# Stage work paced by TensorE time beside a selective scan: equal shares, three slots, two of them ahead of the spread

## The chip, the cores and the metric

The kernel runs on one core of one Trainium2 chip. The metric is the time of one execution in device microseconds; lower is better. The time shown for the kernel before is the median of three executions.

## The reference

The input is `x` of shape (4, 96, 64, 64) in float32: four images of 96 channels. Four layers follow each other, and each computes `x = x + f(group_norm(x))`.

- Layer 0 is an attention of three heads over half-sized samples, with a 3 x 3 neighbourhood part and a 5 x 5 depthwise convolution.
- Layers 1 and 3 hold a two-dimensional selective scan in four directions (rows and columns, forwards and backwards). For 192 channels `d`, 16 states `n` and 4096 positions `t` it computes

```
h[d,n,t] = exp(delta[d,t] * A[d,n]) * h[d,n,t-1] + (delta[d,t] * u[d,t]) * B[n,t]
y[d,t]   = sum over n of h[d,n,t] * C[n,t]
```

  Around the scans stand projections, depthwise convolutions, layer norms and gates.
- Layer 2 is a 3 x 3 sharpening convolution.

## The kernel before, in words

All of it is one program of the function `streams`. Eight scans follow each other, in the order of `SCANS`: layer 1 and layer 3 for each of the four images. Beside each scan, the program computes a *stage* of an image (`BESIDE`): `first` (layer 0 and the front of layer 1), `second` (the rest of layer 1, layer 2 and the front of layer 3), `third` and `last` (the rest of layer 3). The first stage of image 0 runs before all scans. Scans 0, 3 and 4 have a `first` beside them; scans 1, 2, 5 and 6 a `second`; scan 7 has three `third` and the `last`.

**Units.** A scan is cut into groups (a direction, a stretch of 1024 positions, one half of the channels), and a group into 12 units of 8 channels x 16 states = 128 partitions and 1024 positions. There are 8 x 32 x 12 = 3072 units, 384 in each scan. What a unit `i` needs is done by small functions:

- `fetch(i)` (SyncE, SP): a DMA that spreads 8 rows of `dd` (delta) over 128 partitions, into `rep`.
- `decays(i)` (ScalarE): `rep = exp(rep * A)`, line 1952.
- `drive(i)` (TensorE): the *spread*, two bf16 matmuls of 512 columns with a 0/1 matrix `spread`, which put delta * u, held as three bf16 `parts`, on 128 partitions in the PSUM tile `bx`. There are two `bx` tiles, so `drive(i + 2)` can begin when `scan(i)` is done with its own.
- `times_b(i)` (VectorE, line 1965): `bx = bx * B`, in place.
- `scan(i)` (VectorE, line 1972): the recurrence along 1024 positions, into `hs`; `carry_on(i)` (ScalarE, line 1980) keeps its last column.
- `times_c(i)` (GpSimd, line 1984): `rep = hs * C`.
- `collect(j)` (TensorE): for three units at once, the sum over states into the PSUM tile `acc`: 6 float32 matmuls of 32 rows. A unit in which it is issued is called *due*.
- `output(j)` (VectorE or ScalarE, lines 2011 to 2017): takes `acc` to `yo` at a group's end.

`prepare(g)` computes what group `g` needs (`dd`, the products with B and C, and `parts`) while the group ahead of it runs. It is a generator: it issues a piece, then gives control back. The stages are generators too. Their pieces come in pairs: a piece of TensorE work (`yield`), then its *evacuation* from PSUM by ScalarE, VectorE or both (`yield` with a cost). A convolution gives control back between its matmuls, too (`yield (1,)`). All PSUM tiles of stages come from `bank()`: two buffers (`one`), of which `held()` keeps one for as long as a sum needs it.

**The order.** The program's order is written out by hand (`manual_schedule`): each engine executes its instructions in the order in which `unit(i, prep, work, budget)` issues them. `Slots.begin` issues the next piece of a generator, as far as a budget allows; `Slots.end` issues its evacuation. Before the change, the main loop gives each unit a budget in abstract pieces:

```
PACE = {"first": 3.5, "second": 3.7, "third": 3.2}
owed = min(owed, 0.5) + PACE[BESIDE[s][0][0]] - (2.1 if i % 3 == 1 else 0.0)
```

and `unit` issues, in this order: the fetch for unit i + 4; a first slot (preparation, in its first three slots, or else stage work); `decays(i + 2)`; `scan(i)`; `carry_on(i - 1)`; `times_c(i)`; `collect` in a due unit; `drive(i + 2)`; then, if budget is left, the first slot's evacuation and a second slot; `times_b(i + 1)`; `output`; and the remaining evacuations. So the second slot's matmuls stand behind the spread, and where there is a second slot of stage work, the first one's evacuation stands between `scan(i)` and `times_b(i + 1)`.

Near a scan's end, `work.run()` issues what is left of the stage at once.

Of the kernel before, what the change touches and what calls it, by code (L numbers as in the profile page):

```python
# [10 lines left out]
BF16 = mybir.dt.bfloat16  # L11
# [9 lines left out]
R, N = 6, 16  # L21
# [6 lines left out]
CH = 1024  # L28
NCH = L // CH
PCH = 512  # L30
# [8 lines left out]
          (("first", 3),), (("second", 2),), (("second", 3),), (("third", 0), ("third", 1), ("third", 2), ("last", 3)))  # L39
GN_EPS = 1e-5  # L40
PHI_EPS = 1e-12


PHI_SAFE = 10.0
# [850 lines left out]
def streams(ctx: ExitStack, tc: tile.TileContext, x, wts, cst, out, wat, cat, flag):  # L895
# [4 lines left out]
    keep = ctx.enter_context(tc.tile_pool(name="keep", bufs=1))  # L900
# [39 lines left out]
    spread = keep.tile([128, 4, 128], BF16, name="spread")  # L940
# [4 lines left out]
    def img(t):  # L945
        return t.rearrange("p (a b) -> p a b", b=W)

    def mm(o, lhsT, rhs, first=True, last=True):
        nc.tensor.matmul(o, lhsT=lhsT, rhs=rhs, start=first, stop=last)  # L949

    solo = [True]
# [859 lines left out]
              for k, axis, back in KINDS[tag] for c in range(NCH) for h in range(2)]  # L1811
    carry = keep.tile([128, 2, NG], F32, name="carry")
    sums = keep.tile([96, len(SCANS), 4, 2, 2 * NCH], F32, name="sums")
    cuts = [keep.tile([128, 6, PCH], BF16, name=f"parts{n}") for n in range(2)]
    for t in cuts:
        nc.gpsimd.memset(t, 0.0)
    low, ready, live = {}, {}, {}
# [21 lines left out]
    def prepare(g):  # L1839
# [83 lines left out]
        def to_parts():  # L1923
            for q in range(4):
                nc.sync.dma_start(
                    out=parts[32 * q : 32 * q + 24],
                    in_=du[:, :, bass.ts(q % 2, PCH)].rearrange("(s m d) r x -> m (d r) s x", m=2, d=8)[q // 2])

        later(1, to_du)
        later(3, to_parts)  # L1930
# [23 lines left out]
    def drive(i):  # L1954

        g, m = place(i)
        parts = ready[g][0]
        bx = ps.tile([128, CH], F32, tag="bx", name="bx")
        for e in range(2):
            mm(bx[:, bass.ts(e, PCH)], spread[:, 2 * (m % 2) + e, :], parts[:, m // 2, :])  # L1960
        live[i].append(bx)

    def times_b(i):
        bx = live[i][1]
        nc.vector.tensor_mul(bx, bx, ready[i // NG][2][:, 0, :])  # L1965
# [16 lines left out]
    def times_c(i):  # L1982
        a, hs = live[i]
        nc.gpsimd.tensor_tensor(a, hs, ready[i // NG][2][:, 1, :], ALU.mult)  # L1984
# [35 lines left out]
        return lambda: nc.sync.dma_start(out=dst, in_=yo)  # L2020

    AHEAD, BEHIND, LEAD = 4, 2, 6
    PACE = {"first": 3.5, "second": 3.7, "third": 3.2}
    total = len(groups) * NG
    per = total // len(SCANS)
    store, waiting, stored, owed = [], [], [0], 0.0
# [12 lines left out]
    def unit(i, prep, work, budget):  # L2039


        if i + AHEAD < total:
            fetch(i + AHEAD)
        while store:
            store.pop()()
            stored[0] += 1
        catch_up(1)
        j = i - BEHIND - 2
        due = j >= 0 and j % 3 == 0
        first_, rest = (prep, work) if 1 <= prep.slots <= 3 else (work, idle)  # L2050
        budget -= first_.begin(budget)
        if i + 2 < total:
            decays(i + 2)
        scan(i)
        if i:
            carry_on(i - 1)
        times_c(i)
        if due:
            collect(j)
        if i + 2 < total:  # L2060
            drive(i + 2)
        if first_ is work and budget > 0.9:
            rest = work
        if rest is not idle:
            first_.end()
            budget -= rest.begin(budget)
        if i + 1 < total:
            times_b(i + 1)
        if due and j % NG == NG - 3:
            store.append(output(j))  # L2070
        first_.end()
        rest.end()
        if first_ is not prep:
            prep.begin(0)
            prep.end()
        return budget

    class Slots:

# [1 line left out]
        def __init__(self, stage):  # L2081
            self.stage, self.open, self.slots = stage, False, 0

        def begin(self, budget):

            if budget < 0:
                return 0
            self.slots += 1
            used = 0
            v = next(self.stage, 0)  # L2090
            if v == WAIT:
                return budget
            while isinstance(v, tuple):
                used += v[0]
                if used >= budget:
                    return used
                v = next(self.stage, 0)
            self.open = v is None
            return used + (1 if self.open else v)

        def end(self):
            if self.open:
# [16 lines left out]
    with tc.manual_schedule():  # L2119
        for _ in prepare(0):  # L2120
            catch_up(9)
        catch_up(9)
        prep = Slots(prepare(1))
        for _ in range(LEAD):
            prep.begin(0)
            prep.end()
            catch_up(1)
        for i in range(AHEAD):
            fetch(i)
        decays(0)  # L2130
        decays(1)
        drive(0)
        drive(1)
        times_b(0)
        for i in range(total):
            s, at = divmod(i, per)
            g, m = divmod(i, NG)
            if at == 0:
                work, owed = Slots(beside(s)), 0.0
            if m == NG - LEAD and g + 2 < len(groups):  # L2140
                prep.run()
                prep = Slots(prepare(g + 2))

            if at == per - NG - LEAD - 1 and s < len(SCANS) - 1:
                work.run()

            owed = min(owed, 0.5) + PACE[BESIDE[s][0][0]] - (2.1 if i % 3 == 1 else 0.0)
            owed = unit(i, prep, work, owed)
        for j in range(total - 3, total, 3):
            collect(j)  # L2150
            output(j)()
            stored[0] += 1
# [51 lines left out]
```

## Time and profile before

| | |
|---|---|
| time, median of 3 runs | 14,391.75 us (14,391.1 to 14,398.4) |
| profiled execution | 14,400.5 us, span 14,398.6 us |
| granted TensorE clock, mean | 0.866 |
| before the first scan instruction / after the last | 690.6 us / 126.7 us |
| busy: TensorE, VectorE, GpSimd, ScalarE | 84%, 81%, 71%, 61% |
| DMA queue of SP, share of the 16 engines | 73.2% |
| scans 0 to 7, us each | 1632, 1656, 1666, 1634, 1629, 1659, 1669, 2037 |

The page is one execution taken by the profiler. A group's line gives the source line, engine, operation, tiles (written <- read), shapes and count, then busy time in us and the mean duration of one in ns, then idle time of the engine just ahead of these instructions and what ended it. Line 949 is the helper `mm`: all matmuls carry it, and are told apart by their tiles. A line of waits reads: who waited, for whom, us in total, times, longest us. A busy TensorE is not TensorE at its peak, since matmuls are pipelined and the ends of their spans are modelled.

### The profile page before, as it was taken

To read this page: it belongs to the slowest core of one execution; us is meant where nothing else is said; L and a number is where in the kernel's file an instruction comes from. 1 tells how busy PE (TensorE), PEld (TensorE's weight loads), DVE (VectorE), ACT (ScalarE), POOL (GpSimd) and SP (SyncE) were. 2 spreads that over 40 slices of the span, in tenths; PEclk is the share of its full clock that TensorE was granted. 3 is DMA by queue.
4 is the path that set the end of the run, shared out by engine and by line. 5 is a ranking of instruction groups with operands and counts; after the bars stand their busy time and mean duration, and the time that the engine had idled before them with its cause. 6 is when DMAs were issued, how large, how long until landed. Compare 5 with 4: busy or idle time off the path is not lost. (4 is left out here: it accounts for less than half of the span.)

```text
span 14398.6 us, 127507 instructions
## 1 busy us (share of the span) xinstructions
PE 12060.6 (84%) x40149; PEld 3562.9 (25%) x40802; DVE 11655.5 (81%) x7509; ACT 8713.8 (61%) x12340; POOL 10204.6 (71%) x4636
## 2 busy tenths in 40 slices
PE   8888887988889797889878887988979887777776
PEld 2322321322223222222222222222313222111111
DVE  1488898888878888889888898888888888778776
ACT  3266575557756676665766566566756667665554
POOL 0177886877868777778877787777868778666564
PEclk9889997998889897989879898898979888777777
DMA  0277787787877878778877788787877878677674
GB/s 9 64 174 179 193 216 198 187 207 187 223 178 199 205 200 209 180 174 206 223 185 178 186 209 219 176 207 186 212 186 197 209 190 220 168 179 173 161 184 111
DMA packets 902736, 2644.48 MB, mean 184 GB/s; under 512 B 107104, under 2 KB 257088, under 8 KB 902048
## 3 DMA queue, kind: packets, MB, share of 16 engines
q1 hardware_dynamic: 901392, 2634.72, 73.2%
q8 instruction: 324, 5.31, 0.2%
q14 instruction: 364, 2.98, 0.1%
q10 hardware_dynamic: 656, 1.46, 0.0%
HBM read 2169.16 MB, written 466.62 MB: 183 GB/s over the span
## 5 line engine op out<-in xcount | busy, mean ns | idle before, releaser
L1984 POOL TENSOR_TENSOR rep<-hs,bc 128x1024 f32<-128x1024 f32 x3072 | 7221.1, 2356 | 3057.2 <-DVE hs L1972 2499.8
L1972 DVE TENSOR_TENSOR_SCAN hs<-rep,carry,bx 128x1024 f32<-128x1024 f32 x2304 | 5401.7, 2344 | 266.0 <-ACT carry L1980 12.2
L1965 DVE TENSOR_TENSOR bx<-bx,bc 128x1024 f32<-128x1024 f32 x3072 | 3723.7, 1212 | 852.5 <-PE bx L949 432.9
L1952 ACT ACTIVATE rep<-rep,l_decay 128x1024 f32<-128x1024 f32 x3072 | 3495.7, 1143 | 519.9 <-DMA rep<-dd 502.7
L949 PE MATMUL bx<-parts,spread 128*128 128x512 bf16 x5491 | 1938.0, 429 | 1589.5 <-DVE hs L1972 1522.7
L949 PE MATMUL acc<-rep,ct 128*32 128x512 f32 x12288 | 2439.7, 703 | 16.0 <-POOL rep L1984 11.2
L1972 DVE TENSOR_TENSOR_SCAN hs<-rep,bx 128x1024 f32<-128x1024 f32 x768 | 1754.6, 2285 | 139.0 <-ACT carry L1980 47.8
L949 PEld LDWEIGHTS <-spread 128*128 128x128 bf16 x6144 | 426.0, 100 | 4080.5 <-DVE hs L1972 2610.9
L949 PE MATMUL one<-band,dg 96*96 96x512 f32 x2304 | 1048.0, 592 | 4.0
L949 PE MATMUL one<-upad,diag 96*96 96x512 f32 x2016 | 949.2, 607 | 3.8
L949 PEld LDWEIGHTS acc<-rep,ct 128*32 128x32 f32 x12288 | 492.2, 123 | 1676.0 <-issue 1401.2
L949 PE MATMUL one<-qq,kk 96*128 96x512 f32 x1152 | 684.4, 678 | 114.4 <-ACT ex L1288 75.2
L1288 ACT ACTIVATE ex<-one 128x512 f32<-128x512 f32 x576 | 342.4, 594 | 580.4 <-PE one L949 573.9
L949 PE MATMUL one<-pr,ct 6*96 6x512 f32 x1024 | 621.3, 690 | 78.6 <-DVE V L1193 10.4
L1952 ACT ACT_TABLE_LOAD x495 | 635.1, 1283 | 80.5 <-DMA rep<-dd 72.3
L949 PE MATMUL one<-hp,diag 96*96 96x512 f32 x1152 | 578.2, 642 | 31.3 <-POOL diag L1113 28.6
L1980 ACT COPY carry<-hs 128x1 f32<-128x1 f32 x2304 | 408.7, 177 | 287.0 <-DVE hs L1972 285.4
L949 PE MATMUL one<-vpad,diag 96*96 96x512 f32 x1200 | 559.2, 601 | 1.9
L949 PE MATMUL held<-ex,cols 128*32 128x256 f32 x3072 | 518.8, 415 | 8.0 <-ACT ex L1288 1.2
L949 PE MATMUL held<-ex,vT 128*32 128x256 f32 x3072 | 519.1, 415 | 0.0
L949 PEld LDWEIGHTS one<-band,dg 96*96 96x96 f32 x2304 | 374.6, 163 | 489.8 <-issue 423.7
L949 PEld LDWEIGHTS one<-upad,diag 96*96 96x96 f32 x2016 | 336.7, 167 | 438.9 <-issue 378.2
(3421 smaller groups left out, 14154.2 us busy)
## 6 DMA issues: line engine op xcount, KB each, us to landing
rep<-dd SPq DMA_DIRECT2D x3072, 512.0 KB
parts<-du SPq DMA_DIRECT2D x1024, 144.0 KB
bc<-rows SPq DMA_DIRECT2D x256, 512.0 KB
dd<-delta SPq DMA_DIRECT2D x256, 384.0 KB
du<-cut SPq DMA_DIRECT2D x256, 384.0 KB
us<-urow SPq DMA_DIRECT2D x128, 384.0 KB
du<-cut SPq DMA_DIRECT2D x256, 192.0 KB
yrow<-yo SPq DMA_DIRECT2D x128, 384.0 KB
```

The lines of the kernel that those rows point to most:

```text
L949: nc.tensor.matmul(o, lhsT=lhsT, rhs=rhs, start=first, stop=last)
L1288: nc.scalar.activation(last.rearrange("p a b -> p (a b)"), p, AF.Exp, scale=HD**-0.5)
L1952: nc.scalar.activation(a, a, AF.Exp, scale=decay[tag][:, k, NG * h + m : NG * h + m + 1])
L1965: nc.vector.tensor_mul(bx, bx, ready[i // NG][2][:, 0, :])
L1972: nc.vector.tensor_tensor_scan(out=hs, data0=a, data1=bx, initial=carry[:, h, m : m + 1] if c else 0.0, op0=ALU.mult, op1=ALU.add)
L1980: nc.scalar.copy(carry[:, h, m : m + 1], live[i][1][:, CH - 1 : CH])
L1984: nc.gpsimd.tensor_tensor(a, hs, ready[i // NG][2][:, 1, :], ALU.mult)
```

## The change

It has three parts.

- **Budget.** `mm` counts the TensorE time of each matmul at full clock (`spent`). A unit's budget is now a number of microseconds per scan (`PACE`), of which the spread (`DRIVE`) and, in a due unit, the sum (`SUM`) are taken off first. `Slots.begin` takes what its piece really issued, at least 0.5 us for each unit of cost; it issues nothing below 0.3 us of budget, and cuts a convolution where the next matmul would go over it.
- **Order.** A unit has up to three stage slots (preparation takes the place of the first in its first three slots). The first stands where it stood. `times_b(i + 1)` comes right after `times_c(i)`, and only then the first evacuation and the second slot; then `collect` and `drive(i + 2)`; then the second evacuation, the third slot, `output`, and the last evacuation. Where preparation isn't first, it has its slot at the end whatever the budget.
- **Rows.** `parts` changes from [128, 6, 512] to [128, 3, 1024]: four channel groups of 8 on four partition quarters, rather than two groups times two halves of the columns. Its loads have 72 rows of 2048 bytes each where they had 144 of 1024.

```diff
+PACE = (3.08, 3.54, 3.54, 3.08, 3.08, 3.54, 3.54, 3.4)
...
+    spent = [0.0]
+
     def mm(o, lhsT, rhs, first=True, last=True):
+
+        n = 1
+        for d in rhs.shape[1:]:
+            n *= d
+        m = o.shape[0]
+        passes = 1 if rhs.dtype == BF16 else 1.33 if m == 32 else 2 if m == R + 2 * N else 4
+        spent[0] += n * passes / 2400
         nc.tensor.matmul(o, lhsT=lhsT, rhs=rhs, start=first, stop=last)
...
-    cuts = [keep.tile([128, 6, PCH], BF16, name=f"parts{n}") for n in range(2)]
+    cuts = [keep.tile([128, 3, CH], BF16, name=f"parts{n}") for n in range(2)]
...
-                    in_=du[:, :, bass.ts(q % 2, PCH)].rearrange("(s m d) r x -> m (d r) s x", m=2, d=8)[q // 2])
+                    in_=du.rearrange("(s m d) r x -> m (d r) s x", m=4, d=8)[q])
...
-            mm(bx[:, bass.ts(e, PCH)], spread[:, 2 * (m % 2) + e, :], parts[:, m // 2, :])
+            mm(bx[:, bass.ts(e, PCH)], spread[:, m % 4, :], parts[:, m // 4, bass.ts(e, PCH)])
...
-    PACE = {"first": 3.5, "second": 3.7, "third": 3.2}
+    DRIVE, SUM, SLOT = 0.43, 1.71, 0.5
...
         due = j >= 0 and j % 3 == 0
-        first_, rest = (prep, work) if 1 <= prep.slots <= 3 else (work, idle)
-        budget -= first_.begin(budget)
+        left = budget - DRIVE - (SUM if due else 0.0)
+        mine = 1 <= prep.slots <= 3
+        left -= prep.begin(1.0) if mine else work.begin(left)
         if i + 2 < total:
             decays(i + 2)
         scan(i)
         if i:
             carry_on(i - 1)
         times_c(i)
+        if i + 1 < total:
+            times_b(i + 1)
+        if mine:
+            prep.end()
+        work.end()
+        left -= work.begin(left)
         if due:
             collect(j)
         if i + 2 < total:
             drive(i + 2)
-        if first_ is work and budget > 0.9:
-            rest = work
-        if rest is not idle:
-            first_.end()
-            budget -= rest.begin(budget)
-        if i + 1 < total:
-            times_b(i + 1)
+        work.end()
+        left -= work.begin(left)
         if due and j % NG == NG - 3:
             store.append(output(j))
-        first_.end()
-        rest.end()
-        if first_ is not prep:
-            prep.begin(0)
+        work.end()
+        if not mine:
+            prep.begin(1.0)
             prep.end()
-        return budget
+        return left
...
-        def begin(self, budget):
-
-            if budget < 0:
-                return 0
+        def begin(self, left):
+
+            if left < 0.3:
+                return 0.0
             self.slots += 1
-            used = 0
+            t = spent[0]
             v = next(self.stage, 0)
             if v == WAIT:
-                return budget
+                return left
             while isinstance(v, tuple):
-                used += v[0]
-                if used >= budget:
-                    return used
+                if spent[0] - t + 0.4 > left:
+                    return spent[0] - t
                 v = next(self.stage, 0)
             self.open = v is None
-            return used + (1 if self.open else v)
+            return max(spent[0] - t, SLOT * (1 if self.open else v))
...
-            owed = min(owed, 0.5) + PACE[BESIDE[s][0][0]] - (2.1 if i % 3 == 1 else 0.0)
+            owed = min(owed, 0.6) + PACE[s]
             owed = unit(i, prep, work, owed)
```

## The prediction

> **What bounds the kernel now.** I read the busy shares first, then the costliest groups, the stretches, and last VectorE's list of waits.
>
> ```profile
> PE 12060.6 (84%) x40149; PEld 3562.9 (25%) x40802; DVE 11655.5 (81%) x7509; ACT 8713.8 (61%) x12340; POOL 10204.6 (71%) x4636
> ...
> L1972 DVE TENSOR_TENSOR_SCAN hs<-rep,carry,bx 128x1024 f32<-128x1024 f32 x2304 | 5401.7, 2344 | 266.0 <-ACT carry L1980 12.2
> L1965 DVE TENSOR_TENSOR bx<-bx,bc 128x1024 f32<-128x1024 f32 x3072 | 3723.7, 1212 | 852.5 <-PE bx L949 432.9
> ```
>
> There are 3072 units, and each puts one scan (2344 ns) and one product (1212 ns) on VectorE: 3.56 us. From scan start to scan start the median is 3.60 us, the mean 4.42 us (13,581 us from the first scan at 690.6 to the last one's end at 14,271.9). TensorE's 84% is busy time at a clock of 0.87; its work is less than that. So a unit is a VectorE rhythm of 3.60 us with holes in it.
>
> The stretches of three of the eight scans (the first, second and last 384 units):
>
> ```profile
> 690.60:2322.20 1631.60, 1371.11 (x5463) 412.79 (x5556) 1401.11 (x852) 1026.73 (x1490) 1272.62 (x572) 0.87 0.78 195
> 2322.20:3977.90 1655.70, 1423.67 (x4256) 427.90 (x4332) 1403.80 (x868) 1056.92 (x1454) 1268.29 (x571) 0.89 0.79 198
> 12234.50:14271.90 2037.40, 1520.53 (x3861) 365.14 (x3928) 1598.03 (x1132) 1205.34 (x1701) 1267.88 (x593) 0.76 0.69 171
> ```
>
> Columns: stretch, length, busy PE, PEld, DVE, ACT, POOL, granted clock, DMA share. VectorE idles about 230, 252 and 439 us in them. Over all eight, its busy time is 11,446 us, so the holes are 2135 us. What ended them:
>
> ```profile
> DVE bx L1965 <- PE bx L949: 432.9, 281, 11.8
> DVE bx L1965 <- PE acc L949: 350.4, 175, 8.0
> DVE yo L2011 <- PE acc L949: 159.9, 77, 6.6
> DVE V L1193 <- PE one L949: 118.0, 48, 9.9
> DVE x L1600 <- ACT one L1599: 100.3, 32, 6.9
> ```
>
> Summed from the whole list: (A) `times_b` waiting for a late spread, 790 us; (B) `output` waiting for the sum, 215; (C) stage evacuations on VectorE waiting for TensorE, 385; (D) the same waiting for ScalarE, 255; (E) the rest 123. What remains, 367 us, is 0.12 us in each unit ahead of the scan, and stays.
>
> How a spread gets late shows in the timeline of the first scan:
>
> ```profile
> 1005.13 1.09 PE L949 MATMUL one<-pr,ct 6*96 6x512 f32 x2
> 1009.07 2.02 PE L949 MATMUL one<-pr,ct 6*96 6x512 f32 x2
> 1011.02 1.03 PE L949 MATMUL bx<-parts,spread 128*128 128x512 bf16 x2
> 1020.71 1.23 DVE L1965 TENSOR_TENSOR bx<-bx,bc 128x1024 f32<-128x1024 f32 x1 [4.91 <-PE acc L949]
> ```
>
> The same pair takes 1.09 us and then 2.02: the clock has halved. TensorE falls behind and VectorE loses 4.91 us.
>
> **What the Trainium skill says.** "TensorE: Matmul & The Clock Gate", part 3 (packing small matmuls), says matmuls start and end in strict program order: a spread waits for whatever stage matmul stands ahead of it. The trace agrees (the spreads run in issue order). Its part 1 (the HAM clock gate) says too little activity halves the clock. The trace shows the doubling above, and stretches of 24 units with a clock of 1.00 where TensorE has 3.7 to 3.9 us of counted work per unit, but 0.66 where it has 1.2. "DMA: Bandwidth & Descriptors", Specifications, gives 512 B as enough for line rate; here the trace differs: packets of 1024 B take 94 ns, of 2048 B 106 ns, so halving the packet count saves nearly half the time. The measurement decides.
>
> **The change part by part.** I counted each unit's matmuls from the instruction order of both programs, at the change's own rate (512 bf16 columns 0.21 us, a 512-column f32 matmul 0.85 us, a sum 1.71 us). Totals are the same: 1111 us in the first scan, 1215 in the second, 1039 in the last. Matmul, weight-load, VectorE and GpSimd counts are equal; the ScalarE table loads in the program fall by 36 of 4105, at 1.28 us each 46 us of an engine that is 61% busy, so nothing.
>
> 1. *Equal shares.* A unit with a sum has on average 3.73 us of counted work in the second scan and one without 2.88 now; then 3.36 and 3.07. Blocks of 24 units reach 3.9 now, 3.66 then. Units over 4.2 us fall from 14% to 3%. That sits at the 3.60 us rhythm where it used to stand above. In the first scan, whose attention part has the half-clock example, a block's peak drops only from 3.45 to 3.10.
> 2. *Two slots ahead of the spread.* Stage matmuls behind the spread of their unit fall from 239 to 35 us in the first scan, 232 to 41 in the second, 283 to 84 in the last; slots opened there from 153 to 33, 99 to 25, 224 to 83. Now the evacuation of such a slot stands on VectorE right after `times_b`, 1.2 us after the scan's end, while its matmul can only begin after the spread (0.4 to 0.6 us) and takes 0.85 or more: it nearly always waits. In the new order, TensorE does this work while the scan runs.
> 3. *`times_b` ahead of the evacuations.* Today 346 VectorE stage operations, in 252 units, stand between scan and `times_b`; then 4. Each gives its matmul (or TensorE and then ScalarE) 1.2 us more.
> 4. *Rows of 2048 B.* 1024 loads of `parts` at 144 packets become 72. 147,456 x 94 ns / 16 = 870 us of the queue engines becomes 73,728 x 106 / 16 = 490. The page's DMA share is 73%; TensorE waited for `parts` only 40 us in all. Bounds 0 to 40; I take 10.
> 5. *Preparation always takes its slot*, whatever the budget, and its ScalarE part now follows `times_b`; GpSimd gets its part of it no later than before. Cover: `prepare` runs over a group ahead (12 units, some 45 us). Nothing.
> 6. *What the moves put behind a wait.* `collect` and the spread now stand behind slot 2. Where slot 2 needs what slot 1's evacuation frees, the spread waits too. It has a cover of about 3.1 us: it can start when scan i ends, and is needed when scan i+1 ends (3.6 us, less its 0.5). The stores of `yo` and SP's fetches move with their units and wait for no more.
>
> **The sum.** No row shows the new order, so I choose shares between none and all of each group. (A) -40%, as equal shares remove the peaks of the second kind of scan, but not the half clock of attention: -316 (bounds +300, if slot 2 holds up spreads, to -650). (B) -30%: `output` now follows three slots, but its sum stands behind slot 2: -65 (+60 to -170). (C) and (D) -55%: slots behind the spread fall to about a third, and what is left are chains such as the layer norm's root: -352 (-100 to -520). (E) with the rows -20. Together -753. The profiled execution took 14,400.5 us (span 14,398.6); 8.8 above the median of the runs, 14,391.75. So 13,640.
>
> As a check by stages: a second-kind scan would lose 100 of 1656 (its first 48 units from 5.6 to about 4.8 us, the two blocks near 4.7 to about 4.1), a first-kind one 70 of 1632, the last one 150 of 2037: 4 x 100 + 3 x 70 + 150 = 760.
>
> **Rivals.**
> *Only the order helps.* The clock dips of attention decide (A); a slower, even pace leaves TensorE idle more often, so dips don't get rarer. (A) and (B) stay, (C) and (D) give 350: about 14,040. For it: the stall of 4.91 us above came at a block average under 3.3.
> *Nearly all holes close.* A pace below the rhythm with 3.1 us of cover leaves hardly a late spread: (A) -80%, (B) -50%, (C) and (D) -75%: -632, -107, -480, less 30: 13,140. For it: the 24 units from 3884 us on, with little stage work, run at 3.60 us in all but a few. Against it: GpSimd is busy 3.31 us and DMA 3.4 (then about 3.3) per unit, so little is left between four engines.
> *Slower: slot 2 holds the spread.* TensorE stops at slot 2's matmul until slot 1's evacuation frees its bank or writes its operand, and that evacuation now follows `times_b`. 709 units open two or more stage slots. If the wait takes 1.2 us (`times_b`) and one evacuation of 0.7 beyond the cover, 709 x 1.9 = 1350 against -753: 14,990. It decides from 1.06 us a unit on. Against it: most pairs are evacuated by ScalarE, before the scan ends, and depend on an earlier unit.
> *The shares change little.* Stage work is the same, TensorE late as before, and evacuations wait behind `times_b` for as long: 14,390.
>
> **How the numbers follow.** The sum as worked out 0.42 (13,640); only the order 0.24; nearly all holes 0.18; no difference 0.03; slower 0.13. Within 0.2% is what a measurement of this kernel can't tell from no change. Faster 0.84, same 0.03, slower 0.13. The range reaches from the case of most holes closed to the small gain with half of it lost, 13,150 to 14,280; slower than that is left out, as is the better half of the best case.
>
> **What would show it.** In the changed kernel's profile: the median from scan to scan still 3.60 us, the mean about 4.18; VectorE busy unchanged near 11,650 and its share about 86%; its waits for `bx` and `acc` together about 480 instead of 790, those of `V`, `x` and the other stage tiles together under 300 instead of 640; TensorE's idle time before `bx` for `hs` (1522.7) clearly down; the last scan under 1900 us; the clock of the second-kind scans above 0.89; DMA time of 1024 B packets gone. It is wrong if `times_b` waits as long or longer while stage waits fall (dips or slot 2), or if TensorE's waits for stage evacuations ahead of spreads grow by more than 700 us.

## The result and the profile after

The changed kernel takes 14,302.5 us (median of 4 runs, 14,296.3 to 14,315.9), the kernel before 14,392.2 beside it. The ratio is 0.9938, interval 0.9921 to 0.9955: 90 us faster, where 752 had been forecast (13,640, with a range from 13,150 to 14,280). The profiled execution took 14,307.7 us, its span is 14,305.9.

Lines in the changed kernel stand 10 higher in number (the product is L1975, the scan L1982). Busy times, and the two groups that make the rhythm:

```profile
PE 11985.5 (84%) x40137; PEld 3529.3 (25%) x40802; DVE 11649.8 (81%) x7509; ACT 8688.1 (61%) x12304; POOL 10200.4 (71%) x4636
...
L1982 DVE TENSOR_TENSOR_SCAN hs<-rep,carry,bx 128x1024 f32<-128x1024 f32 x2304 | 5401.1, 2344 | 285.5 <-ACT carry L1990 26.2
L1975 DVE TENSOR_TENSOR bx<-bx,bc 128x1024 f32<-128x1024 f32 x3072 | 3721.1, 1211 | 863.1 <-PE bx L959 501.9
```

VectorE's work is the same to a few us, and the median from scan to scan is still 3.60 us. The same three stretches (first, second and last 384 units; columns as before):

```profile
689.20:2337.90 1648.70, 1382.26 (x5467) 409.65 (x5560) 1398.56 (x851) 1026.84 (x1492) 1271.71 (x572) 0.87 0.77 193
2337.90:3975.90 1638.00, 1414.93 (x4254) 425.72 (x4332) 1401.95 (x868) 1053.41 (x1449) 1268.41 (x571) 0.89 0.79 200
12167.00:14178.60 2011.60, 1514.42 (x3860) 355.60 (x3930) 1597.25 (x1132) 1188.93 (x1685) 1266.83 (x593) 0.76 0.69 173
```

The first scan grew by 17 us, the second shrank by 18, the last by 26; the clock reads the same in each of the three. VectorE's waits:

```profile
DVE bx L1975 <- PE bx L959: 501.9, 325, 15.0
...
DVE bx L1975 <- PE acc L959: 220.4, 82, 11.9
DVE x L1610 <- ACT one L1609: 131.9, 31, 6.4
DVE yo L2021 <- PE acc L959: 99.0, 75, 6.8
DVE V L1203 <- PE one L959: 78.5, 35, 7.0
```

The product waits as long as before: its two lines come to 722 us (783 before), but with what the profile puts down to other releasers all its idle time is 833 us (822 before). `yo` and `V` wait less, but `x`, the gate that ends a chain of stage work, waits more. The changed kernel took back in one place what it gained in another, and two stretches of the second scan show it. They are its units 48 to 168 (convolutions over `band`) and 216 to 288 (mostly gates: convolution over `hp`, two projections, multiplication), in the kernel before,

```profile
2590.24:3079.80 489.56, 470.85 (x1478) 155.98 (x1501) 430.27 (x256) 297.89 (x437) 391.51 (x171) 0.98 0.81 200
3279.38:3594.19 314.81, 279.18 (x815) 84.06 (x831) 256.41 (x152) 216.99 (x277) 239.64 (x109) 0.90 0.72 183
```

and in the changed one:

```profile
2596.26:3050.15 453.89, 446.79 (x1433) 148.08 (x1458) 422.38 (x245) 288.58 (x422) 391.96 (x172) 1.00 0.85 210
3255.60:3597.04 341.44, 286.30 (x815) 83.83 (x831) 259.07 (x157) 228.90 (x304) 238.22 (x105) 0.86 0.67 173
```

The convolutions went from 4.08 to 3.78 us a unit and to a clock of 1.00: equal shares do what they should, though a part may come from 3% fewer matmuls in these units (1433 for 1478). The gates, with the same number of matmuls (815), went from 4.37 to 4.74.

One of those gate units, in the timeline of the changed kernel (VectorE's, ScalarE's and the deciding TensorE lines, 3346 to 3356 us):

```profile
3346.88 2.35 DVE L1982 TENSOR_TENSOR_SCAN hs<-rep,carry,bx 128x1024 f32<-128x1024 f32 x1
...
3347.71 0.68 ACT L1597 ACTIVATE x<-one,wt 96x512 f32<-96x512 f32 x1
...
3348.65 1.06 PE L959 MATMUL one<-x,wt 96*48 96x512 f32 x2
3349.14 1.21 DVE L1975 TENSOR_TENSOR bx<-bx,bc 128x1024 f32<-128x1024 f32 x1
3349.35 1.28 ACT L1962 ACT_TABLE_LOAD   x1
...
3350.64 1.15 ACT L1962 ACTIVATE rep<-rep,l_decay 128x1024 f32<-128x1024 f32 x1
...
3351.78 0.68 ACT L1603 ACTIVATE g<-one,wt 48x512 f32<-48x512 f32 x1
...
3352.51 2.02 PE L959 MATMUL one<-g,l_ag 48*96 48x512 f32 x2 [2.80 <-ACT g L1603]
...
3354.46 1.03 PE L959 MATMUL bx<-parts,spread 128*128 128x512 bf16 x2
3354.56 0.65 ACT L1609 ACTIVATE one<-one,der 96x512 f32<-96x512 f32 x1 [2.11 <-PE one L959]
...
3355.25 0.69 DVE L1610 SCALAR_TENSOR_TENSOR x<-one,x 96x512 f32<-96x512 f32 x1 [4.90 <-ACT one L1609]
3355.86 2.33 DVE L1982 TENSOR_TENSOR_SCAN hs<-rep,carry,bx 128x1024 f32<-128x1024 f32 x1
```

Read it backwards from the second scan. It comes 8.98 us after the first, because the multiplication of `x` stands ahead of it on VectorE. That multiplication waited 4.90 us for the `tanh` on ScalarE; this one for the second projection on TensorE; that for `g`; and `g` stood on ScalarE behind a table load (1.28 us) and the decays (1.15). Two projections of one chain were issued in one unit, so VectorE paid for the whole round through TensorE and ScalarE. TensorE stood too (2.80 us), and the spread behind the projection came late. By the time at which they ran, 22 of the 32 second projections stood in one unit with the first in the kernel before, at a mean of 7.66 us a unit, and 31 of 32 in the changed one, at 9.08. A long unit catches more of its neighbours' work, so this is a symptom; how many were issued together is counted further down.

### The profile page after: what moved, and what is told of

Same layout as the page of the kernel before. It is cut to its first block, busy times and chain, and to the rows that moved or that the text cites. A ratio compares the mean times of both kernels' runs of the same rounds, so it can differ in the third digit from the quotient of the medians.

```text
span 14305.9 us, 127489 instructions
## 1 busy us (share of the span) xinstructions
PE 11985.5 (84%) x40137; PEld 3529.3 (25%) x40802; DVE 11649.8 (81%) x7509; ACT 8688.1 (61%) x12304; POOL 10200.4 (71%) x4636
## 4 chain that ended last, share of the span: by engine, by line
PE 45%; DVE 17%; ACT 13%; DMA 8%; POOL 7%; issue 7%; SPq 1%; DVEq 0%; POOLq 0%; ACTq 0%; another core or an unknown queue 0%
PE one L959 28%; DVE hs L1982 10%; PE acc L959 8%; PE bx L959 7%; DVE bx L1975 5%; DMA rep<-dd 4%; POOL rep L1994 4%; ACT rep L1962 3%; PE held L959 2%; ACT L1962 1%; ACT L1904 1%; ACT ex L1298 1%; ACT delta L1902 1%; DMA yc<-ycol 1%; ACT cut L1924 1%
## 5 line engine op out<-in xcount | busy, mean ns | idle before, releaser
L1982 DVE TENSOR_TENSOR_SCAN hs<-rep,carry,bx 128x1024 f32<-128x1024 f32 x2304 | 5401.1, 2344 | 285.5 <-ACT carry L1990 26.2
L1975 DVE TENSOR_TENSOR bx<-bx,bc 128x1024 f32<-128x1024 f32 x3072 | 3721.1, 1211 | 863.1 <-PE bx L959 501.9
L959 PE MATMUL acc<-rep,ct 128*32 128x512 f32 x12288 | 2359.0, 688 | 18.1 <-POOL rep L1994 15.1
L1982 DVE TENSOR_TENSOR_SCAN hs<-rep,bx 128x1024 f32<-128x1024 f32 x768 | 1754.0, 2284 | 102.1 <-ACT carry L1990 22.7
L959 PEld LDWEIGHTS <-spread 128*128 128x128 bf16 x6144 | 456.2, 101 | 3350.5 <-DVE hs L1982 1832.1
```

What stands on the lines that cost most here:

```text
L1982: nc.vector.tensor_tensor_scan(out=hs, data0=a, data1=bx, initial=carry[:, h, m : m + 1] if c else 0.0, op0=ALU.mult, op1=ALU.add)
```

## The experiments

Eighteen kernels follow. The times are medians of 4 to 20 runs, and each ratio is to the kernel before as it ran beside that kernel (14,375 to 14,392 us). The columns after the ratio sum VectorE's idle time from the first scan to the end of the last, every operation of the trace counted (the prediction's groups A to D are sums of list rows, so A is 822 here and not 790): (A) ahead of the product, nearly all of it late spreads, (B) `output`, (C) stage work waiting for TensorE, (D) for ScalarE. Then comes the length of the last scan. The last column counts, in the order of instructions, pairs of stage pieces of which the second needs the result of the first and both are issued in one unit: of 190 pairs, at the eight places that `e13_two_chain` marks, those with both evacuations between the same two `decays` on ScalarE, or the same two scans on VectorE.

| kernel | us | ratio to before | A | B | C | D | last | pairs |
|---|---|---|---|---|---|---|---|---|
| before | 14,392 | | 822 | 220 | 394 | 265 | 2037 | 46 |
| changed | 14,303 | 0.9938 [0.9921, 0.9955] | 833 | 150 | 295 | 310 | 2012 | 122 |
| e1_rows | 14,380 | 0.9992 [0.9984, 0.9999] | 823 | 228 | 391 | 267 | 2036 | 46 |
| e2_order | 14,016 | 0.9742 [0.9725, 0.9760] | 847 | 161 | 169 | 167 | 1867 | 46 |
| e3_budget | 14,445 | 1.0039 [1.0027, 1.0052] | 669 | 230 | 516 | 328 | 2049 | 93 |
| e4_spread_first | 14,560 | 1.0118 [1.0099, 1.0138] | 774 | 196 | 498 | 367 | 2120 | 122 |
| e5_price | 14,280 | 0.9922 [0.9905, 0.9938] | 857 | 181 | 296 | 278 | 1975 | 132 |
| e6_two | 13,998 | 0.9734 [0.9718, 0.9750] | 768 | 186 | 175 | 211 | 1856 | 68 |
| e7_price_two | 14,171 | 0.9852 [0.9835, 0.9868] | 759 | 235 | 202 | 264 | 1852 | 94 |
| e8_free_only | 14,174 | 0.9849 [0.9832, 0.9865] | 877 | 114 | 264 | 235 | 1969 | 111 |
| e9_three_ahead | 14,308 | 0.9942 [0.9926, 0.9959] | 858 | 139 | 284 | 302 | 2001 | 122 |
| e10_two_behind | 14,388 | 0.9995 [0.9988, 1.0002] | 725 | 241 | 474 | 292 | 2043 | 68 |
| e11_two_shares | 14,196 | 0.9866 [0.9849, 0.9882] | 745 | 241 | 199 | 266 | 1862 | 94 |
| e12_two_free | 14,107 | 0.9808 [0.9790, 0.9826] | 840 | 188 | 176 | 199 | 1884 | 89 |
| e13_two_chain | 13,916 | 0.9678 [0.9662, 0.9694] | 765 | 181 | 166 | 166 | 1863 | 0 |
| e14_three_chain | 14,126 | 0.9832 [0.9815, 0.9848] | 713 | 183 | 260 | 262 | 2007 | 4 |
| e15_two_chain_more | 13,930 | 0.9688 [0.9671, 0.9704] | 744 | 223 | 149 | 120 | 1849 | 0 |
| e16_two_high | 14,079 | 0.9796 [0.9780, 0.9812] | 732 | 265 | 164 | 238 | 1850 | 60 |
| e17_three_chain_more | 14,061 | 0.9787 [0.9760, 0.9814] | 717 | 190 | 270 | 179 | 1973 | 0 |
| e18_two_chain_low | 13,876 | 0.9658 [0.9631, 0.9685] | 736 | 161 | 150 | 158 | 1849 | 0 |

In the expectations the letters are theories, which each text explains; the groups of the table are always in brackets here.

### The three parts of the change, one at a time

`e1_rows` is the kernel before with the rows alone:

```
-    cuts = [keep.tile([128, 6, PCH], BF16, ...
+    cuts = [keep.tile([128, 3, CH], BF16, ...
```

> The kernel before with the rows of parts at 2048 bytes and nothing else. All theories: 5 to 15 us less than before (TensorE waited 40 us for parts in all), so 14,380. If the transfers were worth more than their waits, over 40 us.

Measured: 12 us (1 to 23). The rows are worth about what the forecast gave them (10).

`e2_order` is the kernel before with the new order of a unit; it keeps two slots, the old budgets and the old rows:

```
         times_c(i)
+        if i + 1 < total:
+            times_b(i + 1)
...
         work.end()
+        if mine or budget > 0.9:
+            budget -= work.begin(budget)
         if due:
             collect(j)
         if i + 2 < total:
             drive(i + 2)
```

> The kernel before with the new order alone: times_b right behind times_c, and the second slot ahead of the sum and the spread, under the old budgets of at most two slots. Theory 1 (chains: a second piece that reads what the first piece's evacuation writes holds the spread back, TensorE idles and its clock halves): VectorE's waits for stage pieces fall by 100 us or more, its waits for spreads rise by as much or more in chains; 14,350 to 14,550. Theory 2 (clock: dips come from the pace, whatever the order): waits for spreads as before, stage waits down, 14,250 to 14,300. Theory 3 (clumps of pieces without matmuls, let in by their price of 0.5 us): none here, 14,250.

Measured: 376 us faster, more than any of the three theories had. (C) and (D) fall from 659 to 336, (B) by 59. (A) rises by 25.

`e3_budget` keeps the old order and takes only the new prices and equal shares (raised to 3.25, 3.62 and 3.5, so that no work is left over at the end of a scan):

> The new budgets alone, in the old order with two slots (the shares raised to 3.25, 3.62 and 3.5 us so that two slots still empty the stages). Theory 1: the convolutions gain as in the changed kernel (some 200 us of holes), no chain is made worse: 14,150 to 14,230. Theory 2: the even pace brings as many dips as it takes peaks away: 14,350 to 14,450. Theory 3: the clumps are here too, with two slots rather than three: 14,250 to 14,350, with the group norms' units slower than before.

Measured: 53 us slower, which is in the range of theory 2, but not by its mechanism, since the spreads come less late: (A) falls by 153 while (C) and (D) grow by 185; in this order the evacuations stand ahead of the product, and a longer wait there can cover part of a late spread, so the two may not be separate gains and losses. In sum the order gives 376, and with it in place the rest of the change (budgets, third slot and rows) takes 287 back. By the profiles, half of these 287 lie in the first seven scans (143), half in the last (145).

`e4_spread_first` is the changed kernel with the spread ahead of slot 2:

```
         work.end()
-        left -= work.begin(left)
         if due:
             collect(j)
         if i + 2 < total:
             drive(i + 2)
-        work.end()
+        left -= work.begin(left)
+        work.end()
         left -= work.begin(left)
```

> The changed kernel with the sum and the spread moved ahead of the second slot; all else as changed. Theory 1: the spread no longer stands behind a piece that waits, chains fall back to the holes of before, the convolutions keep theirs: 14,050 to 14,200, waits for spreads under 600 us. Theory 2: same as the changed kernel or slower, since late evacuations come back: 14,300 to 14,400. Theory 3: 14,300, the group norm's clumps as in the changed kernel.

Measured: 258 us slower than the changed kernel. Slot 2 does hold some spreads up ((A) falls by 59), but behind the spread its evacuation makes VectorE wait for TensorE ((C) and (D) grow by 260). No theory had it that slow. The rival that slot 2's place ahead of the spread is what costs falls, and that order is right.

### Prices, and the third slot

What in the budgets costs? `e5_price`, `e6_two`, `e7_price_two` and `e8_free_only` vary the least price of a piece, and the number of slots:

```
e5, e7:  -    DRIVE, SUM, SLOT = 0.43, 1.71, 0.5
         +    DRIVE, SUM, SLOT = 0.43, 1.71, 0.85
e6, e7:           drive(i + 2)
         -    work.end()
         -    left -= work.begin(left)
e8:      -    return max(spent[0] - t, SLOT * (1 if self.open else v))
         +    return max(spent[0] - t, SLOT if self.open else 1.2 * v)
```

> The changed kernel with one price raised: a piece of stage work costs at least 0.85 us of the unit's share where it cost at least 0.5 (its smallest cost in the order of the kernel before, whose unit of 1 is worth about 0.85 us); shares 3.14, 3.56 and 3.4 so that no work is left over at the end of a scan. Theory A (clumps: pieces with little TensorE work but long ScalarE or VectorE work were almost free, so chains of them follow one another within a unit): falls at least half way from 14,303 to 14,016, to 14,050 to 14,160; the idle time of VectorE in units of chain pieces (r with l_lin, X with l_c, t with l_c, gate pieces) back to what the kernel with only the new order has. Theory B (the even pace keeps TensorE below the load that its full clock needs): at or above 14,290, since the price hardly moves the counted load. Theory C (the third slot's issue of TensorE work right behind the spread is what costs): above 14,220.

> The changed kernel without its third slot (the last piece, behind the spread); shares raised to 3.24, 3.6 and 3.48 so that nothing is left over at the end of a scan. Theory C: falls to 14,050 to 14,160. Theory A: part of the way, 14,150 to 14,250, since two cheap pieces in place of three still follow each other. Theory B: unchanged within 50 us of 14,303.

> Both: pieces cost at least 0.85 us and no third slot; shares 3.3, 3.62 and 3.5. Theory A: at most 14,100; with the convolutions' VectorE idle time still at the changed kernel's level it could come below the 14,016 of the new order alone, 13,950 to 14,050. Theory B: above 14,280. Theory C: no different from the kernel without the third slot.

> The changed kernel with a higher price for the pieces without a matmul alone (1.2 us times the piece's old cost where it was 0.5 times); pieces with a matmul keep their minimum of 0.5 us; shares 3.14, 3.54 and 3.4. Theory A in the form 'matmul-free pieces were too cheap': as much as raising all minimum prices, 14,050 to 14,160. Theory A in the form 'small matmul pieces with long evacuations were too cheap': above 14,220. Theory B: within 50 us of 14,303.

Measured: the higher price brings 23 us, which the two intervals can't tell from nothing; the third slot's removal 304, below the range of every theory, and (C) and (D) go from 605 to 386. Dearer matmul-free pieces bring 129, a little less than theory A had for them. With two slots, the higher price and its shares *lose* 173, and `e11_two_shares` below, at the same shares with the low price, is within 25 us of it. So it isn't the price of a cheap piece as such: the theory of clumps, as put, falls, and so does theory B, which had no gain from two slots. It looked like the third slot. The last scan, in numbers, in the kernel without it:

```profile
12008.70:13865.10 1856.40, 1445.71 (x3930) 343.79 (x3930) 1588.98 (x1132) 1205.29 (x1698) 1267.82 (x593) 0.80 0.75 188
```

against 2011.60 in the changed kernel: 155 of the 304 us lie here. The shares were raised along with it, so 304 isn't the third slot's alone: against the same changed kernel, the two other sets of shares that were run with two slots (`e11_two_shares`, `e16_two_high`) give 107 and 224.

### Place or number

`e9_three_ahead` begins the third piece ahead of the output sums and the spread; `e10_two_behind` is `e6_two` with its second piece behind them:

```
e9:  +        work.end()
     +        left -= work.begin(left)
              if due:
                  collect(j)
              if i + 2 < total:
                  drive(i + 2)
     -        work.end()
     -        left -= work.begin(left)
e10: -        left -= work.begin(left)
              if due:
                  collect(j)
              if i + 2 < total:
                  drive(i + 2)
     +        left -= work.begin(left)
```

> The changed kernel with the third slot's piece moved ahead of the output sums and the spread; the same pieces at the same prices and shares, up to three in a unit. Theory D (place: a piece issued behind the spread has its matmuls behind it on TensorE, and its evacuation stands ahead of the next scan on VectorE or of the next unit's work on ScalarE, so that these engines wait for the spread each time): at most 14,080, near the 13,998 without the third slot. Theory E (number: three pieces in one unit are too many wherever they stand, because the spread of the next unit but one comes late or ScalarE has too much to do): 14,280 or more; with the spread pushed back behind three pieces it may reach 14,450.

> The kernel without the third slot (13,998), with its second slot moved behind the output sums and the spread; VectorE's product is still ahead of it. Theory D: at least 14,250, as the first kernel, which also had its second piece behind the spread, is at 14,392 and the changed kernel with both later pieces behind it at 14,560. Theory E: within 60 us of 13,998, since there are still at most two pieces in a unit.

> The kernel without the third slot at the minimum price of 0.5 us (13,998), with the shares that the one with prices of 0.85 had (3.3, 3.62 and 3.5 in place of 3.24, 3.6 and 3.48). It splits the 173 us between those two kernels: if the higher shares do it (stage work bunched early in each scan), 14,120 to 14,180; if the price of 0.85 does it, within 40 us of 13,998; if it is only which piece falls into which unit, anything between.

> The kernel without the third slot with matmul-free pieces at 1.2 us times their old cost (13,998 has 0.5 times). With three slots this price gave 129 us. If it gave them by keeping third pieces away, nothing is left to gain here: within 60 us of 13,998. If it gave them by spreading VectorE's and ScalarE's work, it comes below 13,940.

Measured: the third piece costs the same wherever it stands (14,308 against 14,303), so its place isn't the reason. The second piece behind the spread costs 389 ((A) -43, (B) +55, (C) and (D) +380): there, place decides. Work behind the spread is what the old order lost by, and something that comes with the new budgets and their third piece took much of the gain back. Then `e11_two_shares` upset the simple answer "number": 0.06 and 0.02 more in the shares cost 198 us with still two slots, and `e12_two_free` lost 109 where a gain or nothing was expected.

Units sorted by length say where to look. Those over 8 us hold, above the 3.60 of the rhythm, 838 us in the kernel before, 1081 in the changed kernel, 609 with the order alone, 785 in `e6_two` and 893 in `e11_two_shares`. All shorter units together went the other way, from 1671 (before) to 1337 (changed). Among the long ones are units where pieces of one chain meet, like the gate unit above. By the time at which they ran there are 31 of them, of 9.08 us, in the changed kernel, 18 of 7.72 with the order alone, 28 of 7.76 in `e6_two`, 28 of 10.40 in `e11_two_shares`.

The cause can be told from the symptom in the order of instructions, the last column of the table. The old budgets issue 46 dependent pairs in one unit, the new ones with three slots 122. Ten kernels have their second piece ahead of the spread and nothing that keeps chains apart. Among these the time rises with the pairs, from some 14,000 us at 46 to 68 pairs to some 14,300 at 122 to 132, with exceptions of up to 80 us. The two at 94, `e7_price_two` and `e11_two_shares`, have the same pairs of every kind. The gates are not where the number grew: 24 of their 32 pairs of projections are issued in one unit before, after and with the order alone alike, and their units lose 122, 171 and 102 us above the rhythm, so there something else in the unit adds to it. It grew at relu and the linear projection behind it (4 to 28), at the sum over the four quarters (0 to 20), at the projection of `feat` (6 to 18) and at the first gate projection behind its convolution (0 to 11). This count was made after the runs; it forecast none of them.

### Chains within a unit

So the next kernels forbid such pairs. A stage marks a piece that needs the result of the piece just ahead, and such a piece isn't begun in the unit in which the other ended (eight places; fourteen in `e15_two_chain_more` and `e17_three_chain_more`):

```
                 nc.scalar.activation(g1, p[:48], AF.Relu, ...)
                 yield 1
+                yield CHAIN
                 q = bank()
                 mm(q[:96], w["l3_ag2"][:48], g1)
...
-            if left < 0.3:
+            if left < 0.3 or (ahead and self.chained and self.fresh):
                 return 0.0
...
+                if v == CHAIN:
+                    if ahead and self.fresh:
+                        self.chained = True
+                        return spent[0] - t
```

> The kernel without the third slot at the shares 3.3, 3.62 and 3.5 (14,196), in which a piece that needs the result of the piece before it isn't begun in the unit in which that one ended (eight places: the two projections behind relu and the depthwise convolution, the two gate projections, squares and heads, the projection of feat, the two squeeze matmuls, the sum over the four quarters). Theory G (chains of dependent pieces within a unit make the long units): 14,000 to 14,100, with the 8 gate units of each second-kind scan (6.5 to 16 us where x and g both stand in them) below 6 us each. Theory E (only the number of pieces matters): within 40 us of 14,196.

> The changed kernel with all its three slots, in which a piece that needs the result of the piece before it isn't begun in the same unit (the same eight places; shares 3.12, 3.56 and 3.42 in place of 3.08, 3.54 and 3.4 so that nothing is left over). Theory G: at least half of the third slot's 304 us come back, 14,050 to 14,150, and the time in units of over 8 us falls from 1081 to about 850. Theory E: above 14,240.

> As the kernel with two slots and no chains within a unit, with six more places that forbid it (the turned tiles behind their ScalarE copies, the matmuls of the layer and group norms behind the sums, roots and reciprocals that they need); shares 3.3, 3.66 and 3.54. Theory G: another 40 to 120 us below the one with eight places. Against it stands that the 16 turned tiles take a unit each, so the convolutions get less room: up to 50 us above it.

> The kernel without the third slot with shares of 3.36, 3.66 and 3.54 (13,998 at 3.24, 3.6 and 3.48; 14,196 at 3.3, 3.62 and 3.5). If the time follows the share (stage work bunched early in a scan): 14,300 to 14,450. If it follows where pieces of a chain fall among the units: anywhere from 14,000 to 14,250, no trend.

Measured: `e13_two_chain` is 280 us below `e11_two_shares`, which has the same slots and shares. A rule that holds pieces back also moves where all later ones fall, and that alone can be worth 198 us; but with two slots, the three kernels with the rule (13,876 to 13,930, `e18_two_chain_low` below among them) all lie below the three without it at the same least price (13,998 to 14,196). Forbidding chains is thus worth from 82 us, against the best of these, to 280, against the one with equal shares. `e14_three_chain` is 177 us below the changed kernel, with the third slot still there and the shares raised by 0.02 to 0.04: its first seven scans take 194 us less, its last one 5. The gate as `e13_two_chain` runs it (VectorE's lines and the second projection):

```profile
3334.09 2.35 DVE L1991 TENSOR_TENSOR_SCAN hs<-rep,carry,bx 128x1024 f32<-128x1024 f32 x1
...
3336.48 1.09 PE L960 MATMUL one<-g,l_ag 48*96 48x512 f32 x2 [2.27 <-ACT g L1611]
...
3338.30 0.69 DVE L1619 SCALAR_TENSOR_TENSOR x<-one,x 96x512 f32<-96x512 f32 x1 [0.74 <-ACT one L1618]
3338.91 2.33 DVE L1991 TENSOR_TENSOR_SCAN hs<-rep,carry,bx 128x1024 f32<-128x1024 f32 x1
```

The first projection ran in the unit before; the multiplication now waits 0.74 us where it waited 4.90, and the unit takes 4.82 us instead of 8.98. None of the 32 second projections shares a unit with the first any more; all gate units together lose 71 us above the rhythm instead of 171 in the changed kernel and 197 in `e11_two_shares`. Against the units 48 to 168 and 216 to 288 shown above,

```profile
2551.20:3008.86 457.66, 451.36 (x1444) 150.29 (x1470) 423.90 (x246) 288.65 (x420) 391.87 (x172) 1.00 0.85 209
3209.28:3523.58 314.30, 265.48 (x764) 74.68 (x777) 259.40 (x159) 214.55 (x291) 238.35 (x105) 0.85 0.72 186
```

`e13_two_chain` keeps the convolutions' gain (457.66 where 489.56 was before) and gives the gates back (314.30). The units are the same, the stage work in them not quite: its gates lie some 14 units later than in the changed kernel, and the stretch has 764 matmuls for 815. The whole second scan took 1611 us, for 1638 in the changed kernel.

`e15_two_chain_more` is level with `e13_two_chain` where a further gain was expected: six more places bring nothing in sum. `e16_two_high` shows that the shares have no trend (13,998, 14,196, 14,079 at rising shares). What moves with these times is how many pairs meet (68, 94, 60); between 13,998 and 14,079 it doesn't.

> The changed kernel with its three slots and all fourteen places that forbid a chain of pieces within a unit (shares 3.14, 3.58 and 3.44). Theory G for the last scan as well (its norms, turned tiles and squeeze are chains): 13,980 to 14,050, the last scan at 1,880 to 1,930. If the last scan's loss has another cause (its stage work is done too early and the rest waits for stored rows, whatever the chains): 14,090 to 14,150, the last scan within 30 us of 2,007.

> The kernel with two slots and eight places at 13,916, its share beside first-kind stage work 3.26 in place of 3.3. Without chains within a unit, where the pieces fall should matter less: within 30 us of 13,916, where the same kernel with chains moved by 198 us for 0.06 and 0.02.

Measured: `e17_three_chain_more` (14,061) lies between its two forecasts. Its first seven scans take 11,278 us (11,478 in the changed kernel, 11,318 in `e6_two`, 11,261 in `e13_two_chain`), so there the third slot costs next to nothing once chains are kept apart. The last scan falls only from 2,012 to 1,973, where `e6_two` needs 1,856; of these 117 us, 82 lie in (C) and 19 in (D), stage evacuations that wait. In the changed kernel, the first 264 units of this scan take 5.5 us each, then 48 units 3.7, and the rest, which waits for stored rows, 5.2; without the third slot the scan has no such stretch, at a mean of 4.83.

Why three pieces cost more there is open, and `e17_three_chain_more` doesn't settle it. Its rule notes only the end of a piece that has a matmul, so a pair whose first piece has none can still be issued in one unit. In the last scan, 11 of 30 squeezes still stand in one unit with the ScalarE piece whose result they need (17 in the changed kernel, none in `e6_two`). Chains may be the cause here too; that is not shown.

`e18_two_chain_low`, two slots and eight places at a slightly lower share, is the fastest of all: 13,876 us, 499 below the kernel before beside it (14,375), 426 below the changed one. It moved by 40 us for 0.04 in a share where 30 were the most expected; the ratios, 0.9678 and 0.9658, say 29, and their intervals overlap.

## Why the prediction was wrong, step by step

- **The sum behind `times_b` (A), -316.** This failed first: it measured +11. The share of 40% was taken because equal shares would remove peaks. They do so in the convolutions (36 us in one second-kind scan), but two pieces now stand ahead of the spread, and one that waits for ScalarE holds it, as in the gate unit, where TensorE stood 2.80 us. TensorE's waits for stage evacuations grew from 455 to 975 us (759 with the order alone), and keeping chains apart took 120 us of (A) off in `e14_three_chain`. The order alone left (A) at +25. With the order in place, the new shares with two slots (`e6_two`) take 79 off (A) and yet only 18 off the time, of which the rows may be 12. The sum counted TensorE's work ahead of the spread; its waiting stood in a bound (+300) and in a rival, not in the share. What is left of (A) in the best kernels, 736 to 765, wasn't taken apart; first-kind scans, with the attention, still hold 116 to 120 each in `e13_two_chain`.
- **Stage evacuations (C) and (D), -352.** The mechanism was right and its size nearly so, for the order: -323 in `e2_order`, and `e4_spread_first` and `e10_two_behind` put it back by moving a piece behind the spread. The changed kernel kept only 54 of it. The step that failed is "what is left are chains": they were taken for a rest that stays as it was, though three slots and a price of TensorE time alone pack them into fewer units. (D), evacuations waiting for ScalarE, even grew, 265 to 310. The count that was missing is how many dependent pairs are issued in one unit: 46 before, 122 after. Like the matmuls, it can be counted from the order of instructions. Forbidding the pairs at the eight places takes 194 us off the first seven scans, more than the 143 that the rest of the change lost there. The 145 us that it lost in the last scan are not explained.
- **`output` (B), -65.** Measured -70.
- **Rows, 10.** `e1_rows` measured 12: the estimate rested on TensorE's waits for `parts` (40 us in all), and that was right. The saving of 380 us of queue time was not. The 106 ns were those of other loads of 2048 B. In the trace of `e1_rows`, all packets of 2048 B together take 136 ns in the mean; taking the 78,848 others at their 106 ns, as before, the new ones of `parts` come to about 168, an estimate, where those of 1024 B took 94. So the queue time of `parts` fell from 870 to about 775 us. "DMA: Bandwidth & Descriptors", Specifications, in the Trainium skill gives 512 B as enough for line rate; the prediction let its packet times decide against that, but these loads are nearer to it, with 1.8 times the time for twice the bytes.
- **The rival "only the order helps" (14,040)** is near what the order alone gives (14,016), with (A) unmoved as it said. As a forecast of the changed kernel it failed all the same: it left out that the new shares and the third slot could cost anything. Its reason, the clock dips of the attention, wasn't tested by itself: the first scan's clock stayed at 0.87 in the changed kernel and is 0.89 in `e13_two_chain`.
- **The slower rival** failed in its form (`e4_spread_first`), yet named a part of the loss: TensorE stopping at slot 2 until an evacuation of slot 1. It was priced as a wait of `times_b` and an evacuation on VectorE; what stops TensorE in the gate unit shown is a chain through ScalarE, behind decays and a table load.
- **What would show it:** the first sign that was to prove it wrong came, `times_b` waiting as long while stage waits fell. The other, TensorE's waits for stage evacuations up by more than 700 us, didn't: they grew by 520. The second-kind scans lost 18, 18, 17 and 34 us, not 100; the last one 26, not 150.
- **The range** ended at 14,280, 23 us short. (A) at +11 was within its bound (+300), but (C) and (D) at -54 were not (at least -100): no case let the new budgets take back what the order gave.

## What to carry to other kernels

In this kernel, work that fills gaps beside a bound engine has two costs: the time it takes of each engine, and the rounds from engine to engine between its pieces. A budget in one engine's time evens out the first and makes the second worse, because dependent pieces get packed together. Keep two pieces of which one needs the other out of the same turn, and put none whose evacuation the bound engine must run behind a matmul that it could have passed. Such pairs can be counted in the order of instructions. To see what one costs, sort the turns by length and read the longest ones backwards; an average by group hid it here, since short units gained 334 us and long ones lost 243.

## What the runs showed of the hardware

The second projection of a gate, two matmuls of the same shape, took 2.02 us in the gate unit of the changed kernel and 1.09 us in that of `e13_two_chain`; the spread behind the first took 1.03 us, the one ahead of it, at 3348.11, 0.61. The granted clock in the trace explains it: it was 0.50 from 3351.31 to 3358.13 us, where the first pair ran, and 1.00 from 3323.85 to 3337.50, where the second did. The wait just ahead doesn't: at a clock of 1.00, single matmuls of this kind took 0.67 us after waits of 0.15 and of 2.80 us alike, and at 0.50 they took 1.16 after 1.58 and after 4.43. What let the clock fall was not tested; in the gate unit it fell 1.6 us after TensorE had run out of work, but work alone doesn't keep it up: in the kernel before, around the pair of 2.02 us that the prediction shows, it read 0.50 from 1008.42 to 1018.66 us while TensorE was busy for all of these 10.24 us. And where the shares were even (units 48 to 168 of a second-kind scan, 3.8 us each), the granted clock of the 120 units read 1.00, 0.98 before.
